# Two softmaxes of cross-attention on one core: the whole program in another order, V's squares through DRAM, and a new division of the last sums

## The chip, the cores and the metric

The kernel runs on one core of a Trainium2 chip. The metric is the device time of one execution in microseconds (us). All data is fp32.

## The reference

Cross-attention with two sets of keys and values. The queries come from `x`; the first 77 rows of `ctx` are text, the last 77 are image rows, and each set has its own projections and its own softmax:

```
x   (2, 2048, 640)     ctx (2, 154, 1024)     20 heads of 32
q    = heads(x @ Wq.T)
text = softmax(q @ heads(ctx[:, :77] @ Wk.T).T / sqrt(32))    @ heads(ctx[:, :77] @ Wv.T)
ip   = softmax(q @ heads(ctx[:, 77:] @ Wk_ip.T).T / sqrt(32)) @ heads(ctx[:, 77:] @ Wv_ip.T)
out  = merge(text + ip) @ Wo.T + bo + x
```

## The kernel before

**Order.** The whole program is emitted by hand from one list of words, `SCHEDULE` (L551 to L616), which `emit` (L622) interprets word by word. Nothing is reordered afterwards: the order of the words is the order in which each engine, and SP's one DMA queue, gets its instructions. An engine executes in order, so a word that waits holds all later words of the same engine. `@n` after a word names its PSUM bank or half.

**Steps.** A step q = 0..9 is a batch (0 to 4 are batch 0, 5 to 9 are batch 1) and a chunk of 128 channels, that is 4 heads. Each step has two units u = 2q and 2q + 1 of 1024 tokens, and each unit three groups s = 0, 1, 2 of 3, 3 and 2 token tiles of 128. The words of a step:

| word | engine | what |
|---|---|---|
| `q.u.h`, `cq.u.h` | PE, ACT | queries of 512 tokens, 5 matmuls (L191); copied to SBUF with the scale (L201) |
| `k`, `v`, `ck`, `cv` | PE, ACT | projections of keys and values (L132), copied |
| `R`s.u | PE | scores of a group against 154 keys (L223), into half of PSUM |
| `K`s.u | ACT | copies the scores to SBUF (L235) |
| `M`, `S`, `E` | DVE, POOL, ACT | maxima (L261), subtraction (L275), exponential (L281) |
| `D`, `N` | DVE, POOL | sums (L288) with their reciprocals (L290), normalisation (L295) |
| `T` | DVE | transpose in squares of 32x32 (L302) |
| `A.q`, `CA.q` | PE, ACT | attend with V (L311), for the whole step; copied into `aT` (L334, L338) |
| `SQ.c`, `VS.q.half` | DVE, SP | V transposed to squares (L142); squares spread over the partitions (L148), 8 DMAs a half |
| `LX.u.h` | SP | block of 512 tokens of `x`, 1.28 MB (L176); batch 1's blocks take 3 slots in turn, in the order of the LX words |
| `LK`, `LQ`, `LO` | SP | weights |

A group thus goes PE, ACT, DVE, POOL, ACT, DVE, POOL, DVE, and `A.q` needs the T of all six groups of its step. An LX into a slot waits for the queries that read the slot last.

**Output projection.** Batch 0's, by 7 products of sums instead of 8 for most of its size, lies among the steps of batch 1: `W` and `G` are sums of operands on POOL (L380, L410), `m`j.i the products j of block i on PE (L477, L487), `cm`j.i adds them on DVE into `acc` (L502, L508); `o`, `co` do the last 128 channels (L457, L467). Four blocks i share the buffers `acc` and `res`, in five parts. A store of a part (L446, L448) is issued right in the `co` or `cm` that completes it, and the fetch of the residual for the same part of the next block (L438, L440) comes one store later, from the list `due`. `LF` fetches the five parts of block 0.

**Tail.** Batch 1's projection follows A.9. It uses 33 products, each in two halves (`F`, 66 words of one matmul, L835), of sums of weights (`V`, 128x128, L813 and L815) and sums of rows of `aT` (`X`, 128x1024, L821). A suffix names the engine: `.d` is DVE, `.p` is POOL. `Y` adds a bank into an output part on DVE (L779, L781), and each part is stored when its last `Y` is done. `p`, `z` and `yz` do the last 128 channels; `LW` and `LA` load weights and the residual.

Of the kernel before, what the change touches and what calls it, by code (L numbers as in the profile page):

```python
# [20 lines left out]
def kernel(  # L21
# [122 lines left out]
    def spread_v(q, half):  # L144

        for g in range(G * half // 2, G * (half + 1) // 2):
            for r in range(G):
                nc.sync.dma_start(  # L148
                    out=v4s[q % 2][r * D : (r + 1) * D, g].rearrange("p k d -> p (k d)"),
                    in_=squares(q)[g * D : (g + 1) * D],  # L150
                )
# [92 lines left out]
    def exponential_of(u, s, ps):  # L244

        n = GROUPS[s][1]
        for g in range(G):
            for t in range(n):
                for x in range(2):
                    nc.scalar.activation(  # L250
                        rows_of(u, s)[:, t * G + g, x],
                        rows_in(ps[g], n)[:, t, x],
                        AF.Exp,
                        bias=maxs[(u, s)][:, t * G + g, x : x + 1],
                    )

    def maxima(u, s, ps=None):
        n = GROUPS[s][1] * G
        mx = small.tile([P, n, 2], F32, tag=f"mx{n}", name=f"mx_{u}_{s}")
        if ps is None:  # L260
            nc.vector.tensor_reduce(mx, rows_of(u, s), AX.X, ALU.max)  # L261
# [23 lines left out]
    def sums(u, s):  # L285
        n = GROUPS[s][1] * G
        den = small.tile([P, n, 2], F32, tag=f"den{n}", name=f"den_{u}_{s}")
        nc.vector.tensor_reduce(den, rows_of(u, s), AX.X, ALU.add)  # L288
# [1 line left out]
        nc.vector.reciprocal(rden, den)  # L290
# [205 lines left out]
    def take_product(m, b, i, ps):  # L496
        part = {2: (0, 0), 1: (0, 0), 5: (1, 1), 7: (1, 1), 3: (0, 1), 6: (0, 1), 4: (1, 0)}[m]
        t = part_in(sums_of(b, i), *part)
        if m in (5, 3, 4, 1 if b else 2):
            for op in range(2):  # L500
# [4 lines left out]
                if b and m == 4:  # L505
                    nc.sync.dma_start(out=in_dram(outT, b, i, *part)[:, op], in_=t[:, op])
        else:
            nc.vector.tensor_tensor(t, t, ps.rearrange("p (op t) -> p op t", op=2), ALU.add)  # L508
# [369 lines left out]
```

## Time and profile before

| | us |
|---|---|
| median of 3 runs (511.25 to 512.14) | 511.52 |
| span of the profiled execution | 509.3 |

The page gives the profiled execution's time as its span alone; the median lies 2.2 above it.

In that execution the engines were busy for this share of the span: PE 97%, DVE 85%, POOL 81%, ACT 48%. PE's matmul rows are pipelined and their ends are modelled. In the rows below, `PE` is the matmul queue, `PEld` its weight loads, `SPq` SP's DMA queue. A row of a timeline has start, duration, engine, line, operation, output and inputs, and the count of instructions run together; in brackets is the idle time of the engine just before, and what ended it. A row of a table of windows has the window and its length, then for each of PE, PEld, DVE, ACT and POOL the busy time and the number of instructions, then the clock granted to PE (1.00 is full), the share of the DMA engines, and GB/s. A row of a group has busy time, mean duration in ns, and idle time ahead with what ended most of it. Line numbers are those of the kernel before.

### The profile page before, as it was taken

The page shows a single profiled execution, that of the slowest core. Times are in us where ns is not written, and L with a number is a line of the kernel's source. Part 1 is how long each engine was busy: PE and PEld are TensorE (multiplying, and loading weights), DVE is VectorE, ACT ScalarE, POOL GpSimd, SP SyncE. Part 2 cuts the span into 40 slices and gives each one's busy share as a digit, 9 for nine tenths or more (in the row PEclk, how much of TensorE's full clock was granted, in tenths as well). Part 3 has the DMA queues.
Part 4 walks back from the last instruction along what each step waited for, and adds up shares of the span by engine and source line. Part 5 has one row for each costly group of instructions (what it writes and reads, how often), then busy time and mean ns, then how long its engine had stood idle before and what let it go on. Part 6 is the DMA issues. An engine that isn't in the chain of part 4 may idle for free.

```text
span 509.3 us, 9862 instructions
## 1 busy us (share of the span) xinstructions
PE 496.4 (97%) x4114; PEld 292.1 (57%) x4114; DVE 431.5 (85%) x401; ACT 242.8 (48%) x423; POOL 414.3 (81%) x176
## 2 busy tenths in 40 slices
PE   9999999999989999999999999996999999999996
PEld 5657557557458556446655565553666576444442
DVE  0078989989987989977995999799299999999986
ACT  1266657577566567654636544663466453100000
POOL 0078999999997979988998899799399999468750
PEclk9999999999999999999999999997999999999999
DMA  8994050502441554577444724534914022310017
GB/s 272 357 287 134 16 136 11 142 3 71 129 148 42 157 192 141 200 238 250 146 134 146 242 62 155 210 106 134 322 30 124 27 82 64 125 62 1 21 62 268
DMA packets 67468, 69.34 MB, mean 136 GB/s; under 512 B 5472, under 2 KB 47200, under 8 KB 67424
## 3 DMA queue, kind: packets, MB, share of 16 engines
q1 hardware_dynamic: 66704, 68.00, 42.5%
q8 instruction: 32, 0.52, 0.4%
q10 hardware_dynamic: 720, 0.72, 0.4%
q14 instruction: 12, 0.10, 0.1%
HBM read 54.94 MB, written 10.49 MB: 128 GB/s over the span
## 4 chain that ended last, share of the span: by engine, by line
PE 69%; DVE 9%; DMA 8%; POOL 8%; ACT 2%; SPq 2%; issue 1%; DVEq 0%; POOLq 0%
PE bank L191 22%; PE bank L835 11%; PE bank L477 8%; PE bank L223 8%; PE bank L311 6%; PE bank L132 6%; POOL pb L275 5%; PE bank L457 4%; DMA x<-in_x_dram 3%; DVE pb L302 3%; POOL pb L295 3%; PE bank L487 2%; DVE mx L261 2%; DVE den L288 2%; DMA wo_ct<-in_L_xattn_Wo_dram 2%; DMA aT<-in_L_xattn_Wk_ip_dram 2%
## 5 line engine op out<-in xcount | busy, mean ns | idle before, releaser
L275 POOL TENSOR_TENSOR pb<-pb,mx 128x1848 f32<-128x1848 f32 (+1 forms) x60 | 175.6, 2946 | 42.4 <-DVE mx L261 42.3
L295 POOL TENSOR_TENSOR pb<-pb,rden 128x1848 f32<-128x1848 f32 (+1 forms) x60 | 175.6, 2948 | 15.4 <-DVE rden L290 15.1
L191 PE MATMUL bank<-x,wq 128*128 128x512 f32 x400 | 182.5, 606 | 4.8 <-DMA x<-in_x_dram 4.5
L261 DVE TENSOR_REDUCE mx<-pb 128x24 f32<-128x1848 f32 (+1 forms) x60 | 109.3, 1837 | 34.4 <-ACT pb L235 34.4
L191 PEld LDWEIGHTS bank<-x,wq 128*128 128x128 f32 x400 | 75.0, 193 | 92.8 <-issue 82.8
L235 ACT COPY pb<-bank 128x462 f32<-128x462 f32 (+1 forms) x240 | 101.9, 534 | 54.2 <-PE bank L223 53.6
L281 ACT ACTIVATE pb<-pb 128x1848 f32<-128x1848 f32 (+1 forms) x60 | 94.9, 1583 | 68.0 <-POOL pb L275 67.8
L288 DVE TENSOR_REDUCE den<-pb 128x24 f32<-128x1848 f32 (+1 forms) x60 | 110.2, 1836 | 16.3 <-ACT pb L281 16.3
L302 DVE STREAM_TRANSPOSE pb<-pb 128x1920 f32<-128x1920 f32 (+1 forms) x60 | 114.6, 1924 | 0.9 <-POOL pb L295 0.9
L223 PEld LDWEIGHTS bank<-kT,qT 32*128 32x128 f32 x1280 | 47.1, 185 | 27.6 <-issue 20.2
L223 PE MATMUL bank<-kT,qT 32*128 32x154 f32 x1280 | 58.8, 307 | 1.6 <-issue 1.3
L311 PE MATMUL bank<-pb,v 32*32 32x512 f32 x1600 | 55.5, 597 | 0.7 <-ACT pb L235 0.7
L132 PE MATMUL bank<-wo_ct,aT 128*128 128x154 f32 x320 | 46.8, 301 | 0.4 <-DMA aT<-in_L_xattn_Wk_ip_dram 0.3
L132 PEld LDWEIGHTS bank<-wo_ct,aT 128*128 128x128 f32 x320 | 44.3, 192 | 4.7 <-issue 3.5
L311 PEld LDWEIGHTS bank<-pb,v 32*32 32x32 f32 x1600 | 29.8, 103 | 22.3 <-issue 10.1
L201 ACT ACTIVATE qT<-bank 128x512 f32<-128x512 f32 x40 | 23.5, 599 | 29.3 <-PE bank L191 29.2
L457 PE MATMUL bank<-aT,wo_ct 128*128 128x512 f32 x80 | 36.3, 595 | 0.0
L477 PE MATMUL bank<-aT,wo_ct 128*128 128x256 f32 x128 | 32.3, 386 | 0.0
L477 PEld LDWEIGHTS bank<-aT,wo_ct 128*128 128x128 f32 x128 | 23.6, 190 | 7.6 <-issue 4.4
L502 DVE SCALAR_TENSOR_TENSOR acc<-bank,bo_sb,acc 128x256 f32<-128x256 f32 x32 | 13.6, 466 | 14.9 <-PE bank L487 14.8
L457 PEld LDWEIGHTS bank<-aT,wo_ct 128*128 128x128 f32 x80 | 15.0, 190 | 16.8 <-issue 16.4
L781 DVE TENSOR_TENSOR x<-x,bank 128x512 f32<-128x512 f32 x36 | 23.1, 678 | 1.0 <-PE bank L835 0.9
(71 smaller groups left out, 343.0 us busy)
## 6 DMA issues: line engine op xcount, KB each, us to landing
x<-in_x_dram SPq DMA_DIRECT2D x20, 1280.0 KB, 8.4
out_dram<-acc SPq DMA_DIRECT2D x20, 256.0 KB, 2.6
x<-in_x_dram SPq DMA_DIRECT2D x18, 256.0 KB, 5.4
acc<-in_x_dram SPq DMA_DIRECT2D x16, 256.0 KB, 3.7
out_dram<-x SPq DMA_DIRECT2D x15, 256.0 KB, 2.3
v<-vS SPq DMA_DIRECT2D x160, 20.0 KB, 2.6
wq<-in_L_xattn_Wq_dram SPq DMA_DIRECT2D x9, 320.0 KB, 5.3
aT<-in_L_xattn_Wk_dram SPq DMA_DIRECT2D x5, 512.0 KB, 4.5
```

The source lines that it names most:

```text
L132: nc.tensor.matmul(keys_in(out), loaded[n][:, k, :], cT[:, k, :, t, :], start=(k == 0), stop=(k == NCC - 1))
L191: nc.tensor.matmul(pq, wqs[q % 3][:, k, :], xs[place_of(u, h)][:, k, :], start=(k == 0), stop=(k == NC - 1),)
L223: nc.tensor.matmul(ps[g][:, ts(t, 2 * L)], qTs[(u, h)][g * D : (g + 1) * D, ts(st, P)], kT[g * D : (g + 1) * D, c, b].rearrange("p t l -> ...
L235: nc.scalar.copy(keys_of(u, s)[:, :, g], ps[g][:, : n * 2 * L].rearrange("p (n l) -> p n l", n=n))
L261: nc.vector.tensor_reduce(mx, rows_of(u, s), AX.X, ALU.max)
L275: nc.gpsimd.tensor_tensor(rows_of(u, s), rows_of(u, s), maxs[(u, s)].unsqueeze(3).to_broadcast([P, n, 2, L]), ALU.subtract)
L281: nc.scalar.activation(e, e, AF.Exp)
L288: nc.vector.tensor_reduce(den, rows_of(u, s), AX.X, ALU.add)
L295: nc.gpsimd.tensor_tensor(rows_of(u, s), rows_of(u, s), rdens[(u, s)].unsqueeze(3).to_broadcast([P, n, 2, L]), ALU.mult)
L302: nc.vector.transpose(p, p)
L311: nc.tensor.matmul(pa[r][g * D : (g + 1) * D, :], v4s[q % 2][rows, g, k, :], zones[rows, :, g, k, :], start=(k == 0), stop=(k == NK - 1),)
L477: nc.tensor.matmul(part, w_of[m][:, kp, op], t_of(m, b, i)[:, kp], start=(op == kp == 0 and m in (1, 2, 5)), stop=(op == 1 and kp == 1 and ...
```

## The change

1. **A new `SCHEDULE`**, 1064 words for 969. All words of PE and ACT are the same; their order, and which words lie between which, is new all through.
2. **Reciprocals, stores, fetches as words.** `D` is the sums alone and `I` the reciprocal. `st.i.part` and `fe.i.part` are a store and a fetch of batch 0's projection; `co` and `cm` no longer issue them. `LF` moves from the first words to behind A.2.
3. **V's squares through DRAM.** `VW.q` writes the 128x160 square to a DRAM tile of its own, and `VS.q`, 4 DMAs where 16 were, reads it spread over the partitions. There are four square buffers instead of seven. SP issues 187 DMAs instead of 297.
4. **The sums of the tail** have other engines: nine X go from DVE to POOL (I, L, V, G, F, J, W, D, M) and two from POOL to DVE (E, Q), so that POOL has 19 of 25; eight of V's go from DVE to POOL and seven the other way.
5. `E` and `M` have branches for a form without `K` or `S`. All 60 `K` and 60 `S` are in the list, so each group takes the form that it had.

The diff, cut to its core:

```diff
+    dram = ctx.enter_context(tc.tile_pool(name="dram", bufs=1, space=bass.MemoryType.DRAM))
+    scr = [dram.tile([P, LP], F32, name=f"scr_{n}") for n in range(NP)]
...
-    vS0 = [const.tile([P, LP], F32, name=f"vS0_{n}") for n in range(2)]
-    vS1 = const.tile([P, NC, LP], F32, name="vS1")
+    vS = [const.tile([P, LP], F32, name=f"vS_{n}") for n in range(4)]
...
     def squares(q):
         b, c = divmod(q, NC)
-        return vS1[:, c] if b else vS0[c % 2]
+        return vS[2 * b + c % 2]
...
-    def spread_v(q, half):
-
-        for g in range(G * half // 2, G * (half + 1) // 2):
-            for r in range(G):
-                nc.sync.dma_start(
-                    out=v4s[q % 2][r * D : (r + 1) * D, g].rearrange("p k d -> p (k d)"),
-                    in_=squares(q)[g * D : (g + 1) * D],
-                )
+    def write_v(q):
+        nc.sync.dma_start(out=scr[q], in_=squares(q))
+
+    def spread_v(q):
+
+        for r in range(G):
+            nc.sync.dma_start(
+                out=v4s[q % 2][r * D : (r + 1) * D].rearrange("p g k d -> p g (k d)"),
+                in_=scr[q].rearrange("(g d) l -> d g l", g=G),
+            )
...
     def sums(u, s):
...
+    def invert(u, s):
+        n = GROUPS[s][1] * G
         rden = small.tile([P, n, 2], F32, tag=f"rden{n}", name=f"rden_{u}_{s}")
-        nc.vector.reciprocal(rden, den)
+        nc.vector.reciprocal(rden, dens[(u, s)])
...
     def store(b, i, part):
...
-        if b == 0:
-
-            for f in due:
-                fetch(*f)
-            due[:] = [(i + 1, part)] if i + 1 < NHB else []
...
     def store_last(ps, b, i):
...
-        store(b, i, "last")
...
-        if m in (6, 7, 2 if b else 1) or m == 4 and not b:
-            store(b, i, part)
...
+        elif k == "VW":
+            write_v(x)
+        elif k == "st":
+            store(0, x, PARTS[y])
+        elif k == "fe":
+            fetch(x, PARTS[y])
```

Of the list, the places that the prediction speaks of, before and after. Ahead of A.1:

```diff
-"M0.4 v.2.0@1 T1.3 S0.4 q.5.1@3 cv.2.0 K1.4 T2.3 cq.6.0 S2.4 M1.4 E0.4 A.1@1 cq.5.1 D0.4 S1.4 E2.4 "
+"R1.4@1 I1.3 N1.3 T0.3 K1.4 M1.4 S1.4 T2.3 cv.2.0 S0.4 LK.12 LK.11 VW.1 T1.3 E2.4 E1.4 D1.4 q.5.1@3 "
+"cq.5.1 I1.4 N1.4 q.6.0@1 D2.4 cq.6.0 VS.1 E0.4 D0.4 I0.4 A.1@1 N0.4 T1.4 CA.1 I2.4 R0.5@0 v.2.1@4 K0.5 "
```

Ahead of A.4:

```diff
-"q.10.1@4 S0.9 K1.9 M2.9 M1.9 S2.9 E0.9 q.11.0@5 SQ.4 LX.12.0 LO T2.8 VS.4.0 S1.9 E2.9 D0.9 q.11.1@2 "
-"T1.8 N0.9 E1.9 VS.4.1 D2.9 cq.11.0 cq.10.1 D1.9 N2.9 R0.10@1 cq.11.1 R2.10@0 K0.10 T0.9 N1.9 "
-"q.12.0@4 LX.12.1 K2.10 VS.5.0 T2.9 W0 T1.9 R1.10@0 cq.12.0 M0.10 A.4@1 K1.10 LX.14.0 LX.13.1 LQ.8 "
+"LQ.6 N0.9 LO T1.8 SQ.4 LX.12.0 E1.9 N2.9 D1.9 I1.9 cq.11.0 VW.4 R2.10@0 T0.9 T2.9 N1.9 VS.4 K0.10 W0 "
+"T1.9 K2.10 LX.12.1 M0.10 S0.10 q.12.0@4 cq.12.0 M2.10 R1.10@0 K1.10 A.4@1 CA.4 q.12.1@0 M1.10 S2.10 "
```

Ahead of A.7:

```diff
-"M1.15 m4.1 E2.15 D0.15 S1.15 q.17.0@3 T0.14 G5.2 E1.15 co.2 N0.15 cm4.1 cq.16.1 D1.15 R1.16@1 "
-"cq.17.0 LX.18.0 VS.7.1 R0.16@0 K1.16 D2.15 q.17.1@4 N1.15 K0.16 T0.15 N2.15 M0.16 VS.8.1 R2.16@0 "
-"q.18.0@7 K2.16 T1.15 G7.2 S0.16 T2.15 LX.18.1 M2.16 LX.19.0 A.7@0 LX.19.1 E0.16 VS.8.0 M1.16 S2.16 "
+"D0.14 M0.15 m7.1 R1.15@0 cm2.2 N2.14 T2.14 I0.14 K1.15 q.17.0@5 N1.14 S0.15 E0.15 cm7.1 m4.1 q.16.1@4 "
+"o.2@1 T1.14 N0.14 M1.15 S1.15 M2.15 S2.15 T0.14 st.1.1 D0.15 I0.15 N0.15 cm4.1 E1.15 D1.15 cq.17.0 "
+"E2.15 fe.2.1 cq.16.1 R1.16@1 D2.15 I1.15 N1.15 co.2 G7.2 R0.16@0 I2.15 LX.18.0 N2.15 T0.15 VS.8 K1.16 "
+"M1.16 T1.15 K0.16 S1.16 q.17.1@4 st.1.2 cq.17.1 M0.16 S0.16 R2.16@0 T2.15 K2.16 M2.16 S2.16 E1.16 D1.16 "
+"VS.7 I1.16 q.18.0@7 cq.18.0 st.1.3 E0.16 D0.16 I0.16 N1.16 A.7@0 T1.16 m5.2@7 cm5.2 CA.7 N0.16 LX.18.1 "
```

The start of the tail:

```diff
-"V.E.0.p N1.19 T0.19 p.1@4 cm4.3 LA N2.19 T1.19 p.3@6 V.H.0.d T2.19 V.O.0.p V.C.0.p V.A.0.p V.P.0.d "
-"V.G.0.d V.P.1.d A.9@0 V.M.0.d V.U.0.d V.Q.0.d V.T.0.d V.U.1.d V.T.1.p V.J.0.d V.U.2.d V.D.0.d "
-"X.B.d@0 V.X.0.d V.B.0.d V.X.1.p V.M.1.d V.X.2.d X.A.d@1 CA.9 X.I.d@2 F31.1@0 F31.0@1 X.L.d@3 F0.1@0 "
-"X.U.d@4 z.0 V.I.0.d X.S.d@5 F25.0@2 z.3 X.V.d@6 F0.0@1 V.X.3.d Y0.1.11 V.X.4.p F7.1@3 V.S.0.p yz.3 "
-"X.E.p@7 z.2 Y6.0.10 Y0.0.11 F23.1@0 Y2.1.31 F20.0@2 yz.2 V.S.1.p F23.0@1 Y0.1.01 X.Q.p@8 Y6.0.11 "
+"cm4.3 I2.19 N2.19 T1.19 p.1@4 T2.19 V.P.1.p V.G.0.d V.U.0.d V.Q.0.d V.X.0.d V.X.1.d A.9@0 CA.9 st.3.1 "
+"V.X.2.d V.M.1.d X.A.d@1 V.L.0.d V.T.0.d V.E.0.d F31.1@0 X.I.p@2 X.L.p@3 X.Q.d@8 X.U.d@4 F31.0@1 F0.1 "
+"V.X.3.d z.2 Y0.1.11 F0.0 V.T.1.d st.3.0 F25.0@2 V.H.0.p X.J.p@12 X.E.d@7 z.0 V.C.0.d st.3.3 z.1 st.3.4 "
+"st.3.2 LA V.X.4.d Y6.0.10 V.L.1.p yz.2 X.S.d@5 z.3 yz.3 Y0.0.11 F23.1 V.A.0.d yz.0 F25.1@7 Y6.1.10 "
+"F23.0 Y0.0.01 F20.0 Y6.0.11 Y0.1.01 F7.1@3 Y2.1.31 F20.1 F24.0 F1.1 F4.0@6 Y6.1.11 F1.0 V.N.0.d V.U.1.p "
```

More of the change, by code (lines that the diff above doesn't have):

```diff
@@ L63 @@
     SCALE = 1.0 / float(D) ** 0.5
-    DIRECT = {}
     NP = B * NC
@@ L242, in rows_in @@
         return ps[:, : n * 2 * L].rearrange("p (n t l) -> p n t l", n=n, t=2)
[L244 to L255, printed above, removed]
     def maxima(u, s, ps=None):
@@ L260, in maxima @@
         if ps is None:
-            nc.vector.tensor_reduce(mx, rows_of(u, s), AX.X, ALU.max)
+            nc.vector.tensor_reduce(mx, rows_of(u, s), AX.X, ALU.max, negate=by_rows(u, s))
         else:
@@ L277, in subtract, with exponential, copied, by_rows @@
         )
-    def exponential(u, s):
-        e = keys_of(u, s).rearrange("p n g l -> p (n g) l")
-        nc.scalar.activation(e, e, AF.Exp)
-    rdens = {}
+    def exponential(u, s, ps):
+        if not by_rows(u, s):
+            e = keys_of(u, s).rearrange("p n g l -> p (n g) l")
+            nc.scalar.activation(e, e, AF.Exp)
+            return
+        n = GROUPS[s][1]
+        for g in range(G):
+            for t in range(n):
+                for x in range(2):
+                    row = rows_of(u, s)[:, t * G + g, x]
+                    nc.scalar.activation(
+                        row,
+                        row if copied(u, s) else rows_in(ps[g], n)[:, t, x],
+                        AF.Exp,
+                        bias=maxs[(u, s)][:, t * G + g, x : x + 1],
+                    )
+    def copied(u, s):
+        return f"K{s}.{u}" in planned
+    def by_rows(u, s):
+        return f"S{s}.{u}" not in planned
+    dens = {}
     def sums(u, s):
         n = GROUPS[s][1] * G
-        den = small.tile([P, n, 2], F32, tag=f"den{n}", name=f"den_{u}_{s}")
-        nc.vector.tensor_reduce(den, rows_of(u, s), AX.X, ALU.add)
+        dens[(u, s)] = small.tile([P, n, 2], F32, tag=f"den{n}", name=f"den_{u}_{s}")
+        nc.vector.tensor_reduce(dens[(u, s)], rows_of(u, s), AX.X, ALU.add)
+    rdens = {}
+    def invert(u, s):
+        n = GROUPS[s][1] * G
         rden = small.tile([P, n, 2], F32, tag=f"rden{n}", name=f"rden_{u}_{s}")
-        nc.vector.reciprocal(rden, den)
+        nc.vector.reciprocal(rden, dens[(u, s)])
         rdens[(u, s)] = rden
@@ L440, in fetch @@
             nc.sync.dma_start(out=part_in(acc, *part), in_=in_dram(xT, 0, i, *part))
-    due = []
     def store(b, i, part):
@@ L504, in take_product @@
                 )
-                if b and m == 4:
-                    nc.sync.dma_start(out=in_dram(outT, b, i, *part)[:, op], in_=t[:, op])
         else:
             nc.vector.tensor_tensor(t, t, ps.rearrange("p (op t) -> p op t", op=2), ALU.add)
-        if m in (6, 7, 2 if b else 1) or m == 4 and not b:
-            store(b, i, part)
     slices.extend((i, k) for i in range(NHB) for k in range(NC))
@@ L551 @@
     SCHEDULE = (
[64 rows of a table removed]
[66 rows of a table added]
     ).split()
     late = [tuple(int(x) for x in w.split(".")[1:]) for w in SCHEDULE if w[:2] == "LX"]
+    planned = {w.partition("@")[0] for w in SCHEDULE}
     JOINS = {3: 5, 6: 1, 7: 6, 4: 7}
@@ L636, in emit @@
             square_v(x)
+        elif k == "VW":
+            write_v(x)
         elif k == "VS":
-            spread_v(x, y)
+            spread_v(x)
         elif k == "LX":
@@ L649, in emit @@
                 fetch(0, part)
-        elif k[0] in "KMSEDNT":
+        elif k[0] in "KMSEDINT":
             ps = at[f"R{i}.{x}"]
@@ L653, in emit @@
                 take(x, i, ps)
-            elif k[0] in "ME":
-                direct = (x, i) in DIRECT
-                if k[0] == "M":
-                    maxima(x, i, ps if direct else None)
-                elif direct:
-                    exponential_of(x, i, ps)
-                else:
-                    exponential(x, i)
+            elif k[0] == "M":
+                maxima(x, i, None if copied(x, i) else ps)
+            elif k[0] == "E":
+                exponential(x, i, ps)
             else:
-                dict(S=subtract, D=sums, N=normalise, T=transpose)[k[0]](x, i)
+                dict(S=subtract, D=sums, I=invert, N=normalise, T=transpose)[k[0]](x, i)
         elif k == "q":
@@ L785, in add_part @@
             nc.sync.dma_start(out=outT[ts(m, P), ds(S + i * TB, TB)], in_=t)
-    home = {}
+    home = {step_of(u)[3] * NH + h: xs[place_of(u, h)] for u, h in late[-XROOM:]}
     def finish(k, args, where):
@@ L796, in finish @@
         elif k == "LA":
-            for u, h in late[-XROOM:]:
-                home[step_of(u)[3] * NH + h] = xs[place_of(u, h)]
             (fourth,) = set(range(NHB)) - set(home)
```

104 rows, old and new, of the table SCHEDULE are left out of this document.

## The prediction

> **What bounds the kernel now.** I read the page first, then a table of the span by stages, then the chain and the timelines.
>
> ```profile
> span 509.3 us, 9862 instructions
> PE 496.4 (97%) x4114; PEld 292.1 (57%) x4114; DVE 431.5 (85%) x401; ACT 242.8 (48%) x423; POOL 414.3 (81%) x176
> 140.00:152.80 12.80, 11.48 (x206) 7.55 (x205) 11.40 (x9) 8.51 (x12) 12.80 (x6) 0.96 0.49 147
> 152.80:165.50 12.70, 12.70 (x97) 10.46 (x98) 9.62 (x8) 7.96 (x16) 9.29 (x4) 0.91 0.15 42
> 203.70:216.40 12.70, 11.91 (x96) 5.89 (x106) 11.99 (x10) 7.90 (x15) 12.62 (x6) 1.00 0.57 201
> 343.70:356.40 12.70, 8.85 (x29) 3.81 (x28) 12.67 (x8) 4.57 (x9) 12.37 (x6) 0.73 0.44 134
> 356.40:369.20 12.80, 12.77 (x208) 8.19 (x208) 2.76 (x4) 5.73 (x13) 4.56 (x2) 1.00 0.92 321
> ```
>
> PE is busy 97% of the span: it is the bound, and its words are the same before and after (order apart). Time can come only from stretches in which PE stands or is slow. Three stand out: 140–165, 203–217 and, by far the largest, 343–356 (8.85 busy of 12.70, clock 0.73). DVE and POOL are nearly as full there (12.67, 12.37); only behind the third hole do they stand (2.76 and 4.56 of 12.80), so there they waited for PE and can follow a PE that comes sooner. The chain and the PE queue name the holes:
>
> ```profile
> 150.13 1.32 issue
> 341.48 9.30 DMA x<-in_x_dram
> 350.82 7.34 PE L191 MATMUL bank<-x,wq 128*128 128x512 f32 x10 [3.85 <-DMA x<-in_x_dram]
> 373.94 4.49 PE bank L191 x10
> 358.16 5.45 PE bank L311 x148
> 216.26 5.84 PE L311 MATMUL bank<-pb,v 32*32 32x512 f32 x160 [0.70 <-ACT pb L235]
> 222.77 2.81 PE L191 MATMUL bank<-x,wq 128*128 128x512 f32 x6 [0.67 <-DMA x<-in_x_dram]
> ```
>
> **Load LX.18.0 (the large hole).** It was issued at 341.48, when queries q.17.0 had let go of the slot, took 9.30, and q.18.0 stood 3.85 for it; the queries then ran 7.34 instead of 4.49 at the low clock. That is 3.85 + 2.85 = 6.7. In the new order q.16.1, o.2 and m4.1 are issued between q.17.0 and q.18.0 beside the scores: two pieces of 4.49 (373.94 shows one of that size) and a shorter one more, so that 18.5 us of PE words lie between slot and use, where 7.1 lay (the words' durations in the PE queue, added up). A load of 9.3 fits with 9.2 to spare: **−6.7**. The other late loads keep 10.5 to 12.6 of such room: covered by the same load with 1 us or more to spare; if one took 14, it would cost 2.
>
> **V's squares through memory, and A.4.** Before, each half is 8 DMAs from the squares; now one write and 4 reads. The nearest rows:
>
> ```profile
> 200.88 15.29 SPq L148 DMA_DIRECT2D v<-vS  x16
> out_dram<-acc SPq DMA_DIRECT2D x20, 256.0 KB, 2.6
> v<-vS SPq DMA_DIRECT2D x160, 20.0 KB, 2.6
> 183.84 3.29 POOL L275 TENSOR_TENSOR pb<-pb,mx 128x1848 f32<-128x1848 f32 x1 [2.02 <-DVE mx L261]
> 213.98 2.18 DVE L302 STREAM_TRANSPOSE pb<-pb 128x1920 f32<-128x1920 f32 x1 [0.61 <-POOL pb L295]
> ```
>
> Sixteen issues held SP's queue 15.29, so LX.12.1 behind them was late (0.67 at 222.77), and A.4 ran 5.84 where 358.16 shows 5.45 (0.39). The new chain for A.4 is the square (0.5), a write (2.6, from the larger store), four issues (under 1 each by 15.29/16, together 2 to 4) and a landing (2.6): 7.7 to 9.7, against 8 us of DVE work between SQ.4 and T1.9. It just fits, or costs up to 1.7; I take 0, since the 128x160 write is a third of the store. The 0.70 stood for T1.9, which waited 0.61 for POOL's N1.9; G5.0 is a new word ahead of N1.9, of 1.3 (as at 231.31, below), but it comes ahead of S1.8, where POOL stood 2.02 for DVE, so it costs nothing. I let 0.70, 0.39 and 0.67 all go: **−1.8**. Bounds: −1.8, and +1.2 if the squares are late by 1.7 and G5.0 adds its 1.3.
>
> **Words moved ahead of the last transpose before an attend step.** DVE now has M1.2 before A.0, M1.4 before A.1, M1.16 before A.7; POOL has S2.4 before A.1, G5.1 and S2.12 before A.5, G7.2 before A.7. Queued behind them are the T and N that the attend waits for.
>
> ```profile
> L261 DVE TENSOR_REDUCE mx<-pb 128x24 f32<-128x1848 f32 x40 | 81.7, 2052 | 30.9 <-ACT pb L235 30.9
> L275 POOL TENSOR_TENSOR pb<-pb,mx 128x1232 f32<-128x1232 f32 x20 | 45.1, 2257 | 3.6 <-DVE mx L261 3.6
> 231.31 1.29 POOL L410 TENSOR_TENSOR x<-aT 128x512 f32<-128x512 f32 x1
> 101.95 3.56 DVE L302 STREAM_TRANSPOSE pb<-pb 128x1920 f32<-128x1920 f32 x2
> 106.59 1.92 PE L311 MATMUL bank<-pb,v 32*32 32x512 f32 x49
> 347.28 3.55 DVE L302 STREAM_TRANSPOSE pb<-pb 128x1920 f32<-128x1920 f32 x2
> 225.86 3.29 POOL L295 TENSOR_TENSOR pb<-pb,rden 128x1848 f32<-128x1848 f32 x1 [1.13 <-DVE rden L290]
> 239.13 1.27 POOL L410 TENSOR_TENSOR aT<-aT,x 128x512 f32<-128x512 f32 x1 [1.39 <-PE bank L477]
> ```
>
> A.1: T ended at 101.95 + 3.56 = 105.51, A.1 began at 106.59, slack 1.08; 2.05 more ahead gives +1.0, and 0.1 for A.0: **+1.1**. A.5: POOL has 1.29 + 2.26 = 3.5 more ahead, and idle spells of 1.13 and 1.39 to put it in; 1.0 is left, half of it under A.5's own slack: **+0.5** (0 to 1.7). A.7: T ended at 350.83; without the hole A.7 would start at 358.16 − 6.7 = 351.46, slack 0.63. M1.16 adds 2.05, so 1.4; G7.2 another 1.3 if POOL is what is late. Against it, DVE's queue was full of words that now lie after A.7: **+1.0** (0 to 2.7). A.9 has V.D, V.P, V.M on POOL for V.E, two sums more of 0.44 (row 463.40 below): **+0.3** (0 to 0.9).
>
> **Reciprocals, stores, fetches as own words.** Same instructions, other places. The first residual fetch (5 DMAs) leaves the crowded start for the time after A.2, where the DMA share is 0.15: 0. Stores no longer sit at the end of cm; a store waiting on SP holds the loads behind it, which is the third rival.
>
> **The tail (after A.9).** Sums X (128x1024) go from DVE to POOL 9 times and back 2 times: 19 on POOL, where 12 were; POOL's tail work becomes 49, DVE's 57 where it was 66.
>
> ```profile
> 438.65 5.52 PE L311 MATMUL bank<-pb,v 32*32 32x512 f32 x160
> 444.50 1.98 PE L835 MATMUL bank<-x,wo_ct 128*128 128x512 f32 x4 [0.34 <-ACT aT L338]
> 458.50 46.85 PE bank L835 x108
> 505.38 0.69 DVE x L781
> L821 DVE TENSOR_TENSOR pb<-aT 128x1024 f32<-128x1024 f32 x6 | 7.2, 1216 | 0.0
> L821 POOL TENSOR_TENSOR pb<-aT 128x1024 f32<-128x1024 f32 x3 | 7.1, 2361 | 0.0
> 472.08 2.02 DVE L815 TENSOR_TENSOR pb<-pb,wo_ct 128x128 f32<-128x128 f32 x1
> 459.55 0.28 DVE L815 TENSOR_TENSOR pb<-pb,wo_ct 128x128 f32<-128x128 f32 x1
> 471.61 2.35 POOL L821 TENSOR_TENSOR pb<-pb 128x1024 f32<-128x1024 f32 x1
> 459.90 3.12 POOL L815 TENSOR_TENSOR pb<-pb,wo_ct 128x128 f32<-128x128 f32 x2 [1.59 <-DVE pb L815]
> 463.40 0.87 POOL L815 TENSOR_TENSOR pb<-pb,wo_ct 128x128 f32<-128x128 f32 x2
> ```
>
> An X costs 1.22 on DVE and 2.36 on POOL. Worse, the engines stop each other: a sum of 0.28 on DVE took 2.02 while POOL's X ran from 471.61 to 473.96, and ended when that ended; two POOL sums that take 0.87 (463.40) took 3.12 beside DVE's. From A.9 to the last sum now: 505.38 + 0.69 − 438.65 = 67.4, of which PE stands little. In the new order, with N2.19's end as zero: X.I holds POOL from 0.45 to 2.8 and keeps DVE's V.G off till 2.8; DVE's run of sums to X.A and V.E lasts to 6.9 and keeps X.L off; X.L ends at 9.2, X.Q (DVE) at 10.4, X.U, V.X.3 and Y0.1.11 at 12.6, V.T.1 at 12.9, or 15.0 if POOL's X.J comes first. PE wants V.T.1 for F25.0 at 1.6 (end of T2.19) + 5.52 + 0.34 + 5 words of 0.87 (2 × 46.85/108) = 11.8. It stands 1.1 to 3.2 there; then F23.0 1.6 to 2.6 for Y0.0.11, behind X.E and X.S; F20.1 and F1.1 0.5 to 1.5. What one stall takes the next need not: 4.3 to 6.3 together, less the 1.2 of such waits before: **+4.0** (3.1 to 5.1), and −1.0 if the sums did not stop each other, since DVE then has 9 us less to do.
>
> The Trainium skill, "SBUF — State Buffer", section "SBUF: two separate sides", says that a VectorE instruction with two SBUF inputs and a GpSimd instruction that reads SBUF take turns at one port pair, the later waiting for the whole of the other. By that the tail is the +4.0; by a view in which both merely run at their speeds it is −1.0.
>
> **The gap at 150.** 1.32 without a wait, then a low clock: 12.8 × 0.04 + 12.7 × 0.09 = 1.7, together 3.0. PE's order there is unchanged, so I keep it; if it goes, −3.0. The Trainium skill, "TensorE: Matmul & The Clock Gate", section "Part 1: The HAM clock gate", wants about 3.4 us of idleness before the clock halves; the windows show 0.96 and 0.91 behind 1.32, so here the measurement decides. By the page the stalls of the tail would cost no clock.
>
> **Sum.** −6.7 − 1.8 + 1.1 + 0.5 + 1.0 + 0.3 = −5.6; tail +4.0; total −1.6. Span 509.3 − 1.6 = 507.7. The median before, 511.52, lies 2.2 over the profiled span; with it **509.9**.
>
> **Rivals.**
> 1. *The engines do not stop each other in the new tail, or the gap at 150 is gone.* For it: in most of the old tail's sums the price is 0.28 and 1.22. Against it: rows 472.08 and 459.90. Tail −1.0: 504.9; gap gone: 506.9; both: 501.9. Chance 0.20.
> 2. *The added words cost their upper ends:* A.5 1.7, A.7 2.7, A.9 0.9, that is 3.4 more: 513.3. For it: DVE and POOL are full up to the hole (12.67, 12.37). Against it: 10 us of DVE idleness right behind it. Chance 0.12.
> 3. *Slower: a load waits on SP behind a store.* In the new list LX.18.0 stands behind st.1.1 (which waits for DVE's cm7.1) and fe.2.1 (which waits for that store). DVE is full there; if cm7.1 comes more than 9.2 us late against m7.1 and the fetch, q.18.0 waits again. From 12 us of lateness on, all of 6.7 is back: 509.9 + 6.7 = 516.6; LX.19.1 is behind stores likewise. For it: the row below, 9.8 of SP's waiting for one such product each nine times. Against it: before, the same stores stood ahead of loads and the hole came from PE's slot. Chance 0.14.
> 4. *The tail's stalls bring the low clock as at 150:* two or three spells of 1.7 give 513.3 to 515.0; chance 0.08.
>
> ```profile
> SPq L448 <- DVE acc L508: 49.8, 9, 9.8
> ```
>
> **How the numbers follow.** Forecast 0.46, with a range of its own of 507.5 to 512.0 (the bounds of the terms, not all at one end). A difference of 0.2% (1.0 us) is about what a measurement of this kernel tells from none: faster is below 510.5, slower above 512.5. Faster: 0.31 of the forecast's 0.46 and rival 1's 0.20: 0.51. Same: 0.13 of the forecast and 0.03 of rival 2: 0.16. Slower: 0.02, 0.09, 0.14 and 0.08: 0.33. The range 501.5 to 516.5 leaves out about half of rival 3, and what is beyond rival 1.
>
> **What would show it.** Right: no DMA wait ahead of L191 near 340–350 and PEclk 1.00 there; no PE wait at A.4; A.1 1 us behind its T; POOL's 128x1024 sums beside DVE sums of 128x128 that take 1 to 2.4, and PE standing over 4 us in the first 15 us after A.9. Wrong: a load's wait ahead of L191 past A.6, a tail under 67 us, or PE waits for T of 2 us and more at A.2, A.3, A.6 or A.8, to which I gave nothing.

## The result, and the profile after

The new kernel is slower: 513.03 us median of 19 runs (511.89 to 515.83) against 510.99 us of the kernel before on the same chips (508.68 to 513.09), a ratio of 1.0048 (95% interval 1.0033 to 1.0063; the ratio and its interval are worked out over all executions, not from the two medians). Forecast was 509.9 against 511.5, 1.6 us less; it is 2.0 us more. In the two profiled executions both halves moved further than forecast: up to A.9 the new kernel won 8.9 us where 5.6 were expected, and the tail (from A.9 to the last Y) lost 12.4, 79.8 for 67.4, where 4.0 were expected. Two of the twelve executions of experiment 7 were slow ones, over 6 us longer than the others, and are left out of its numbers.

The busy time of the engines of the kernel after (span 512.4), and the windows that answer to those of before, with three of its tail (same columns):

```profile
PE 496.0 (97%) x4114; PEld 291.5 (57%) x4114; DVE 434.6 (85%) x393; ACT 243.4 (47%) x423; POOL 432.3 (84%) x184
140.00:152.80 12.80, 11.62 (x213) 7.85 (x212) 11.56 (x10) 8.88 (x13) 12.69 (x5) 1.00 0.80 250
152.80:165.50 12.70, 12.68 (x96) 9.17 (x95) 11.65 (x10) 8.32 (x16) 12.08 (x6) 1.00 0.21 54
343.70:356.40 12.70, 12.70 (x197) 7.48 (x197) 10.88 (x9) 8.38 (x16) 12.70 (x5) 1.00 0.75 255
436.10:450.70 14.60, 10.21 (x22) 3.90 (x22) 14.60 (x17) 1.11 (x5) 11.58 (x6) 1.00 0.05 18
450.70:463.10 12.40, 8.87 (x21) 3.77 (x21) 12.37 (x14) 0.00 (x0) 12.08 (x9) 0.97 0.11 42
463.10:470.50 7.40, 7.40 (x10) 3.09 (x11) 3.79 (x6) 0.00 (x0) 2.34 (x2) 0.58 0.11 38
```

The hole at 343.7 is gone (12.70 of 12.70 at full clock). New holes lie in the tail: PE is busy 10.21 of 14.60 and 8.87 of 12.40, and then runs at 0.58 of its clock for 7.4 us. DVE is busy without a break in the first two. PE's queue in the tail:

```profile
429.74 5.52 PE L325 MATMUL bank<-pb,v 32*32 32x512 f32 x160 [0.27 <-DVE pb L316]
436.10 1.96 PE L840 MATMUL bank<-x,wo_ct 128*128 128x512 f32 x4 [0.84 <-ACT aT L352]
441.90 1.13 PE L840 MATMUL bank<-aT,pb 128*128 128x512 f32 x2 [1.27 <-DVE pb L820]
447.43 1.13 PE L840 MATMUL bank<-aT,pb 128*128 128x512 f32 x2 [0.97 <-DVE x L786]
450.72 1.12 PE L840 MATMUL bank<-aT,pb 128*128 128x512 f32 x2 [2.17 <-DVE x L786]
463.08 2.05 PE L840 MATMUL bank<-aT,pb 128*128 128x512 f32 x2 [3.51 <-DVE acc L786]
464.92 3.62 PE L840 MATMUL bank<-pb,wo_ct 128*128 128x512 f32 x4
```

A.9 starts at 429.74 (438.65 before). The waits are those of F25.0 (1.27), F25.1 (0.97), F23.0 (2.17) and F6.0 (3.51), each for DVE; four products behind the last take 3.62 where four took 1.96. DVE and POOL at the same time (L818 and L820 are sums V, L826 sums X, L786 words Y):

```profile
439.66 2.19 DVE L820 TENSOR_TENSOR pb<-pb,wo_ct 128x128 f32<-128x128 f32 x1
443.63 2.43 DVE L820 TENSOR_TENSOR pb<-pb,wo_ct 128x128 f32<-128x128 f32 x1
451.45 1.39 DVE L786 SCALAR_TENSOR_TENSOR x<-x,bo_sb,bank 128x512 f32<-128x512 f32 x2
456.11 4.78 DVE L820 TENSOR_TENSOR pb<-pb,wo_ct 128x128 f32<-128x128 f32 x2
460.81 1.47 DVE L826 TENSOR_TENSOR x<-aT 128x1024 f32<-128x1024 f32 x1
...
451.36 2.36 POOL L826 TENSOR_TENSOR pb<-aT 128x1024 f32<-128x1024 f32 x1
455.99 2.40 POOL L826 TENSOR_TENSOR pb<-pb 128x1024 f32<-128x1024 f32 x1
458.35 2.39 POOL L826 TENSOR_TENSOR x<-aT 128x1024 f32<-128x1024 f32 x1
```

V.T.1 (439.66) takes 2.19 beside POOL's X.J, V.X.4 (443.63) 2.43 beside X.F. V.U.2 and V.V.0 (456.11) take 4.78 for two, while POOL runs X.V, X.T, X.N and X.C one behind the other: each of the two ends 0.15 behind the end of an X (X.N at 458.39, X.C at 460.74). The two Y words at 451.45, which read a PSUM bank and one tensor in SBUF, take 0.70 each beside an X of POOL: they are not stopped. Y0.0.00, for which F6.0 waits, stands behind V.V.0 and X.B.

### The profile page after: what moved, and what is told of

Read it like the earlier page. It is cut to its first block, busy times and chain, and to the rows that moved or that the text cites. A ratio compares the mean times of both kernels' runs of the same rounds, so it can differ in the third digit from the quotient of the medians.

```text
span 512.4 us, 9752 instructions
## 1 busy us (share of the span) xinstructions
PE 496.0 (97%) x4114; PEld 291.5 (57%) x4114; DVE 434.6 (85%) x393; ACT 243.4 (47%) x423; POOL 432.3 (84%) x184
## 4 chain that ended last, share of the span: by engine, by line
PE 84%; DVE 10%; DMA 3%; issue 1%; SPq 1%; POOL 0%; ACT 0%; ACTq 0%; DVEq 0%; POOLq 0%
PE bank L194 32%; PE bank L226 10%; PE bank L325 10%; PE bank L840 9%; PE bank L483 9%; PE bank L133 8%; PE bank L464 3%; PE bank L493 2%; DVE pb L820 2%; DMA x<-in_x_dram 2%; DMA aT<-in_L_xattn_Wk_ip_dram 2%; DVE pb L316 1%; DVE pb L826 1%; DVE mx L251 1%; DVE den L297 1%
## 5 line engine op out<-in xcount | busy, mean ns | idle before, releaser
L194 PE MATMUL bank<-x,wq 128*128 128x512 f32 x400 | 178.8, 598 | 0.1
L226 PE MATMUL bank<-kT,qT 32*128 32x154 f32 x1280 | 57.3, 306 | 1.5 <-issue 1.2
L133 PEld LDWEIGHTS bank<-wo_ct,aT 128*128 128x128 f32 x320 | 43.0, 188 | 4.3 <-issue 2.7
L325 PEld LDWEIGHTS bank<-pb,v 32*32 32x32 f32 x1600 | 31.2, 103 | 22.6 <-issue 10.0
L840 PE MATMUL bank<-aT,pb 128*128 128x512 f32 x36 | 19.2, 645 | 7.9 <-DVE acc L786 3.5
```

Source lines behind the costliest of these rows:

```text
L133: nc.tensor.matmul(keys_in(out), loaded[n][:, k, :], cT[:, k, :, t, :], start=(k == 0), stop=(k == NCC - 1))
L194: nc.tensor.matmul(pq, wqs[q % 3][:, k, :], xs[place_of(u, h)][:, k, :], start=(k == 0), stop=(k == NC - 1),)
L226: nc.tensor.matmul(ps[g][:, ts(t, 2 * L)], qTs[(u, h)][g * D : (g + 1) * D, ts(st, P)], kT[g * D : (g + 1) * D, c, b].rearrange("p t l -> ...
L325: nc.tensor.matmul(pa[r][g * D : (g + 1) * D, :], v4s[q % 2][rows, g, k, :], zones[rows, :, g, k, :], start=(k == 0), stop=(k == NK - 1),)
```

## The experiments

Theory: the tail lost its time because DVE's sums and POOL's row sums stop each other. Rivals: the time won ahead of A.9 is a debt that falls due in the tail; or the order of the F and Y words makes the waits, whoever does the sums; and for the win, that it was LX.18.0's slot. Ratios are to the kernel before on the same chip. Line numbers are those of each kernel: in those of the experiments L843 and L849 are F, L789 Y, L823 V, L829 X, and L836 the fill.

**1. Whose is the loss?** The new kernel with the old tail (the lists are joined behind N0.19; the stores of block 3 ahead of `LA`):

```diff
-"... V.M.0.p p.2@7 D2.19 T0.19 cm4.3 I2.19 N2.19 T1.19 p.1@4 T2.19 V.P.1.p V.G.0.d ..."
+"... V.E.0.p N1.19 p.2@7 D2.19 T0.19 p.1@4 cm4.3 I2.19 st.3.1 ... LA N2.19 T1.19 V.H.0.d T2.19 V.O.0.p ..."
```

> The new kernel up to the last attention step, then the order and the engines of the old tail. Theory (the 12.4 us that the tail got longer, 79.8 against 67.4, come from its own order and engines): A.9 stays near 430 us and the tail comes back to 67 to 68, so 512.4 - 12 = about 500 of span, and a ratio to the kernel before of about 0.98. Rival (the time won ahead of A.9 is a debt of DVE and POOL that falls due in the tail, whoever does the sums): the tail stays at 75 or more, and the ratio at 0.995 or above.

Measured: 503.43 us, ratio 0.9869 (0.9824 to 0.9914). A.9 starts at 432.21, the tail is 68.2, and PE's waits in it are 0.56 ahead of F31.1 and 0.28 later, none of those above; the window of the tail in which the new kernel stood:

```profile
445.00:457.00 12.00, 11.94 (x28) 5.04 (x27) 11.81 (x19) 0.00 (x0) 10.40 (x7) 1.00 0.17 66
```

The debt falls: with an A.9 6.4 us earlier than before, the old tail is only 0.8 longer than it was. The ratio is a little above the 0.98 expected; in the profile A.9 came 2.5 later than in the new kernel's, by a longer pause in A.3 (last section). This version beats both kernels.

The other way round, the kernel before with the new tail, in two forms. In the first, as the old program gives the late blocks their buffers only at `LA`, which comes later in the new tail, sums ahead of it go to another buffer and are lost; the second gives them from the start.

```diff
-"... V.E.0.p N1.19 T0.19 p.1@4 cm4.3 LA N2.19 T1.19 p.3@6 V.H.0.d T2.19 V.O.0.p ..."
+"... N1.19 T0.19 p.1@4 cm4.3 V.M.0.p N2.19 T1.19 p.3@6 T2.19 V.P.1.p V.G.0.d V.U.0.d ..."
```

> The kernel before up to A.9, then the new tail. Theory: the tail is about 12 us longer on its own, so 511 + 12 = 523, ratio about 1.024. Rival (debt): with the old, later A.9 DVE and POOL are not behind, the tail is 67 to 72 and the ratio 1.00 to 1.01.

> The kernel before up to A.9, then the new tail, with the buffers of the late blocks known from the start as in the new kernel. Theory (the tail is 12 us longer on its own): ratio 1.02 to 1.027 to the kernel before, tail 77 to 80. Rival (debt): ratio 1.01 or below.

Measured: 522.3 us, ratio 1.0236 (1.0186 to 1.0287), tail 76.9; and 520.05 us, ratio 1.0162 (1.0122 to 1.0202), tail 78.4 in its profile. In both the waits at F25.0, F25.1, F23.0 and F6.0 are there, the first three as long as in the new kernel to 0.02 us, though A.9 comes 10 us later. The tail's loss is its own. The second ratio is below the 1.02 to 1.027 expected, though. By ratios the two halves are smaller than by the two profiles: the new order ahead of A.9 is worth about 1.3% (6.7 us), and the new tail costs 1.6% on the old list and 1.8% on the new one (1.0048 against 0.9869), 8 to 9 us; by the intervals each of these is known to about 2 us.

**2. Engines, or order?** Each X on the engine that it had, at its new place:

```diff
-... X.I.p@2 X.L.p@3 X.Q.d@8 ... X.J.p@12 X.E.d@7 ... X.F.p@11 ... X.G.p@10 X.V.p@6 ...
+... X.I.d@2 X.L.d@3 X.Q.p@8 ... X.J.d@12 X.E.p@7 ... X.F.d@11 ... X.G.d@10 X.V.d@6 ...
```

> The new kernel, each sum X on the engine that it had before, at its new place in the list (nine back on DVE, two back on POOL); the sums V as in the new one. Theory (sums of DVE and of POOL with two inputs in SBUF stop each other, and POOL's X of 2.36 hold up DVE's of 0.28): most of the 12 us comes back, PE's waits of 1.27, 2.17 and 3.51 go, ratio 0.982 to 0.990. Rival (the order of the F and Y words makes the waits): the waits stay, and DVE has 9 us more to do: ratio 1.01 or above.

Measured: 517.76 us, ratio 1.0151 (1.0094 to 1.0208); tail 79.1. In this form the theory falls, and the ratio is the rival's. PE's queue has other waits, of 9.2 together where the new kernel has 8.8; two of them:

```profile
446.10 1.12 PE L843 MATMUL bank<-aT,pb 128*128 128x512 f32 x2 [2.08 <-DVE pb L823]
465.84 2.08 PE L843 MATMUL bank<-pb,wo_ct 128*128 128x512 f32 x2 [3.35 <-DVE pb L829]
```

F25.0 waits longer for V.T.1, which is still stopped by POOL (now by X.E; it took 1.77); F18.0 waits for X.V, which now stands in DVE's queue behind Y words. The new order needs its engines: X words stand where POOL would start them early. Engines and order were one design, and undoing one of them alone says nothing on the other; whether the order alone makes the waits is left to the next experiment.

**3. POOL's sums short, all else the same.** Each X of POOL does 128 of its 1024 columns:

```diff
+nc.gpsimd.tensor_tensor(places[w][:, :, :64], ra[:, :, :64], rb[:, :, :64], op)
```

> The new kernel, but each X of POOL does 128 of its 1024 columns only (the rest of the sum is left out; same order, same waits). Theory: DVE's sums V.U.0, V.T.1, V.X.4, V.U.2, V.V.0, which took 1 to 2.4 us beside POOL's X, take 0.28 to 0.7, PE's waits in the tail go, tail 67 to 69, ratio about 0.98. Rival (DVE's own amount and order of work): the same instructions of DVE take as long as in the new kernel and PE's 3.51 wait stays.

Measured: 501.28 us, ratio 0.9833 (0.9788 to 0.9879), tail 67.1, PE's four long waits gone. DVE's V.T.1, then V.U.2 with V.V.0:

```profile
438.55 0.28 DVE L820 TENSOR_TENSOR pb<-pb,wo_ct 128x128 f32<-128x128 f32 x1
449.17 0.76 DVE L820 TENSOR_TENSOR pb<-pb,wo_ct 128x128 f32<-128x128 f32 x2
```

2.19 became 0.28 and 4.78 became 0.76, in the same order of words. PE's only waits from A.9 on are 0.26 at A.9 and 0.31 ahead of F31.1. So it is POOL's time in X that holds DVE's sums of other data, and the order by itself does not make the waits.

**4. The stop by itself.** In the idle first 25 us of the new kernel, sums on buffers that nobody else uses:

```diff
+dve_sums(4)                       # 128x128, two SBUF inputs, alone
+start_pool(); 2 x POOL tensor_tensor 128x1024; dve_sums(4)
+start_pool(); 2 x POOL tensor_tensor 128x1024; 4 x DVE tensor_scalar; 4 x DVE SBUF + PSUM
+start_pool(); 2 x POOL tensor_scalar 128x1024; dve_sums(4)
```

> The new kernel with a measurement ahead of its list, in the first 25 us, where DVE and POOL stand: DVE sums of 128x128 from two SBUF inputs alone; the same beside POOL sums of 128x1024; then DVE's one-input products and sums of a PSUM bank and an SBUF input beside POOL sums; then DVE's two-input sums beside a POOL product with one SBUF input. Theory (an engine's whole instruction keeps the other's out): 0.28 alone; beside POOL's sums the first one takes up to 2.4, or POOL's takes 1 us longer; one-input and PSUM forms stay at 0.2 to 0.35 and POOL's at 2.36. Rival (both are slowed in proportion): each DVE sum takes 0.4 to 0.6 in all forms and POOL's over 2.6.

DVE's queue, then POOL's:

```profile
3.70 1.27 DVE L564 TENSOR_TENSOR acc<-acc,res 128x128 f32<-128x128 f32 x4
5.28 4.49 DVE L564 TENSOR_TENSOR acc<-acc,res 128x128 f32<-128x128 f32 x4 [0.31 <-POOL acc L560]
10.14 4.29 DVE L575 TENSOR_SCALAR acc<-acc 128x128 f32<-128x128 f32 x4 [0.38 <-POOL acc L560]
16.17 1.98 DVE L564 TENSOR_TENSOR acc<-acc,res 128x128 f32<-128x128 f32 x4 [0.38 <-POOL acc L560]
...
5.32 3.97 POOL L569 TENSOR_TENSOR acc<-acc 128x1024 f32<-128x1024 f32 x2
10.19 3.91 POOL L573 TENSOR_TENSOR acc<-acc 128x1024 f32<-128x1024 f32 x2
16.22 5.72 POOL L580 TENSOR_SCALAR acc<-acc 128x1024 f32<-128x1024 f32 x2
```

Four sums take 1.27 alone and 4.49 beside two POOL sums, although no datum joins them. One by one they are 0.29, 1.87, 1.94 and 0.29 us: the first runs, the next two each end 0.15 behind the end of a POOL sum. That is a stop until the other's instruction ends, not a slowing in proportion. The theory was wrong for one-input products: they are stopped as well (0.23, 1.80, 1.94, 0.23). That does not hold for every instruction with one input: the 40 maxima `M` of 128x1848 in the new kernel take 2.02 to 2.08 each, with a POOL instruction beside them or not. The PSUM form began at 14.55, when POOL had ended at 14.10, so this run says nothing on it; the row at 451.45 above does.

The last group does not fit the theory. Beside POOL products with one SBUF input, of 2.87 and 2.77, DVE's four sums took 0.29, 1.01, 0.29 and 0.29: the second was held, but not to the end, and the last two began and ended (17.54 to 18.16) while POOL's first product was still running by its row (16.22 to 19.10). Why is open; no X or V of POOL is such a product. The rule of the Trainium skill, "SBUF — State Buffer", section "SBUF: two separate sides", that of a VectorE instruction with two SBUF inputs and a GpSimd instruction that reads SBUF the later waits for the whole of the other, agrees with the rows of two-input sums beside POOL's sums; this last group does not agree with it.

**5. Two sums moved.**

```diff
-V.U.2.d V.V.0.d
+V.U.2.p V.V.0.p
```

> The new kernel with two of the tail's 62 weight sums and row sums, V.U.2 and V.V.0, on POOL instead of DVE. On DVE they took 4.78 us together beside POOL's run of four X, ahead of the word Y0.0.00 that F6.0 waits for. Theory (each two-input sum of DVE that meets a POOL sum waits for the whole of it, and two such waits make F6.0 late): Y0.0.00 comes over 4 us earlier, the wait of 3.67 ahead of F6.0 goes and with it the slow products behind it; the waits ahead of F25.0, F25.1 and F23.0 stay at 4.9 together; tail 72 to 74, ratio to the kernel before 0.990 to 0.995. Rival (POOL is late then, or X.B is stopped in their stead by as much): the wait at F6.0 stays over 2 us, ratio above 1.000.

Measured: 508.38 us, ratio 0.9943 (0.9915 to 0.9972), tail 73.6. The wait at F23.0 is still there, 2.18. F29.0 and F6.0 on PE, and X.B on DVE:

```profile
458.94 1.99 PE L843 MATMUL bank<-aT,pb 128*128 128x512 f32 x4
...
455.66 3.37 DVE L829 TENSOR_TENSOR x<-aT 128x1024 f32<-128x1024 f32 x1
```

F6.0 follows F29.0 without a wait, though X.B is now stopped in their stead (3.37 instead of 1.47). Two instructions of 0.3 us each on the other engine are worth 1% of the kernel: slower than before becomes faster than before.

**6. Seventeen sums V moved** (I, G, X, M, T, E, C, A, U.2, V.0, S, F to `.p`; DVE keeps five of the sums V, and six X):

> [...] Theory: the waits at F25.0, F25.1 and F23.0 (4.9 together) shrink to under 2 as well, tail 68 to 71, ratio 0.984 to 0.990. Rival (POOL, with 7.7 us more to do, is now late with T, X or the row sums): waits of 5 or more, ratio 0.998 or above.

Measured: 507.95 us, ratio 0.9927 (0.9900 to 0.9954), tail 72.8: between the theory and its rival, and no better than two alone.

```profile
446.13 2.13 PE L843 MATMUL bank<-aT,pb 128*128 128x512 f32 x4 [1.39 <-POOL pb L823]
449.77 1.13 PE L843 MATMUL bank<-aT,pb 128*128 128x512 f32 x2 [1.50 <-DVE x L789]
```

The wait at F25.0 is 0.3 now and F25.1 has none, so the three are under 2 together, as expected; but F23.1 waits 1.39 for POOL's sums, which is the rival's mechanism, and F23.0 still 1.50 for Y0.0.11.

**7. The low clock.** Four products of a zero matrix fill the pause ahead of F6.0:

```diff
-F29.0 F6.0
+F29.0 fill fill fill fill F6.0
```

> The new kernel with four PE products more, of a matrix of zeros, between F29.0 and F6.0, where PE stood 3.51 us and then ran at half its clock for 6.9 us. Theory (half of that loss is the clock, which falls because PE stands): PE has no pause there, the products after it take 0.86 instead of 1.70, 3.2 us come back: ratio to the kernel before about 0.9985 where the new kernel has 1.0048. Rival (the clock falls anyway, or the fall is not paid since DVE's Y words are what is late): ratio 1.003 to 1.007.

Measured: 512.3 us (median of ten), ratio 1.0035 (1.0009 to 1.0062).

```profile
458.31 3.60 PE L836 MATMUL bank<-aT,vS 128*128 128x512 f32 x8
462.93 1.88 PE L849 MATMUL bank<-pb,wo_ct 128*128 128x512 f32 x4
```

In this profile the products behind F6.0 run at full clock (four in 1.88 instead of 3.62) and the tail is 76.7 for 79.8: the 3.1 expected. The ratio does not show it: it is the rival's, and its interval covers the new kernel's own. The profiled execution is the fastest of the ten, and one of two whose mean granted clock is 1.000. In three of the five profiles with the new tail and no fill the low clock came behind F23.0 instead, the pause at F6.0 was 2.0 instead of 3.5, and the tail was 76.9, as long as with the fill. So the 3.1 is what the low clock cost in one profile; where it falls differs between executions, and what it costs the median stays open.

**8. The win: slot or store?** In the kernel before, q.17.0 ahead of q.16.1, and then LX.18.0 also ahead of `co.2` in the list:

```diff
-q.16.1@5 K1.15 cm7.1 ... S1.15 q.17.0@3 T0.14 G5.2 E1.15 co.2 N0.15 cm4.1 cq.16.1 D1.15 R1.16@1 cq.17.0 LX.18.0
+q.17.0@3 K1.15 cm7.1 ... S1.15 q.16.1@5 T0.14 G5.2 E1.15 co.2 N0.15 cm4.1 cq.16.1 D1.15 R1.16@1 cq.17.0 LX.18.0
```

```diff
+q.17.0@3 K1.15 cm7.1 ... S1.15 LX.18.0 q.16.1@5 T0.14 G5.2 E1.15 co.2 N0.15 cm4.1 cq.16.1 D1.15 R1.16@1 cq.17.0
```

> The kernel before with one exchange: q.17.0 ahead of q.16.1, so that 4.4 + 2.6 us of PE work more lie between the slot that it frees and q.18.0. Theory (the hole of 6.7 us is LX.18.0's wait for its slot): the hole goes, A.7 starts 6 to 7 us earlier, ratio about 0.987. Rival (A.7 then waits for its transposes, T ending at 350.8): the gain is under 2 us, ratio 0.996 or above.

> The kernel before with q.17.0 ahead of q.16.1 as in the exchange tried before, and the load LX.18.0 in the list right behind it, ahead of the store of co.2, where SP's queue stood from 333 to 341 for DVE. Theory (it was that store, not the slot, which made the load late): the load is issued at about 333.5, the hole of 6.7 us ahead of A.7 goes, ratio about 0.987. Rival (A.7 then waits for its transposes): gain under 2 us, ratio above 0.996.

Measured: 512.22 us, ratio 1.0043 (1.0017 to 1.0070), the hole as it was; and 506.77 us, ratio 0.9897 (0.9858 to 0.9935). Of the first, DVE's `co.2`, SP's queue, and q.18.0:

```profile
340.36 0.71 DVE L467 SCALAR_TENSOR_TENSOR res<-bank,bo_sb,res 128x512 f32<-128x512 f32 x1
341.09 0.36 SPq L446 DMA_DIRECT2D out_dram<-res  x1
343.43 0.34 SPq L438 DMA_DIRECT2D res<-in_x_dram  x1
343.82 0.45 SPq L176 DMA_DIRECT2D x<-in_x_dram  x1
352.91 6.26 PE L191 MATMUL bank<-x,wq 128*128 128x512 f32 x10 [3.96 <-DMA x<-in_x_dram]
```

The slot was free 10 us ahead of the load: SP stood for DVE's `co.2` to store `res`, then for that store to fetch into `res` again. Of the second, the load and q.18.0, which now follows the scores without a wait; then q.17.0 in the kernel before, and in the new kernel q.17.0 and the load:

```profile
335.43 0.37 SPq L176 DMA_DIRECT2D x<-in_x_dram  x1
350.90 4.56 PE L191 MATMUL bank<-x,wq 128*128 128x512 f32 x10
...
335.51 4.46 PE L191 MATMUL bank<-x,wq 128*128 128x512 f32 x10
...
321.59 4.56 PE L194 MATMUL bank<-x,wq 128*128 128x512 f32 x10
326.18 0.37 SPq L179 DMA_DIRECT2D x<-in_x_dram  x1
```

So in the kernel before two things held the load: the slot, until 339.97, and the store with its fetch, until the load's own issue at 341.48. Freeing the slot alone won nothing; freeing it and putting the load ahead of the store won the hole. The load ahead of the store in the old order of the queries was not tried; by these rows it could go only 1.5 us earlier. In the new kernel the load goes at 326.18, when q.17.0 has just ended (326.15): there the slot decides, and no store does.

**9. V's squares straight from SBUF**, at the places of the new list (16 DMAs for a write and four reads). As the squares of batch 1 are written over before they are spread there, their contents are those of other steps; the DMAs are all there.

```diff
-VW: write to DRAM; VS: 4 reads
+VS: 16 DMAs vS -> v
```

> The new kernel with the squares of V spread straight from SBUF by 16 DMAs a step, as before, at the places of the new list. Theory (the way through DRAM frees SP's queue: 4 issues of 0.7 to 1.3 us where 16 took 15): loads behind the squares come late, and 1 to 4 us are lost at q.12.1 or later: ratio 1.006 to 1.013. Rival (no one waits for SP there): the same as the new kernel, 1.003 to 1.006.

Measured: 519.34 us, ratio 1.0141 (1.0102 to 1.0181). A.9 starts 8.1 later than in the new kernel; A.4 and q.19.1 by PE's queue:

```profile
214.35 7.34 PE L325 MATMUL bank<-pb,v 32*32 32x512 f32 x160
393.19 8.82 PE L194 MATMUL bank<-x,wq 128*128 128x512 f32 x20 [2.67 <-DMA x<-in_x_dram]
```

A.4 takes 7.34 for 5.52, for squares that arrive late (its weight loads wait for them four times, 0.44 to 0.63 each), and A.7 takes 7.33. The load that is 2.67 late stood on SP behind 16 issues that took 11.36, as the theory has it, though far behind q.12.1. So the way through DRAM is worth 5 us by the ratios (1.0141 against 1.0048), in the new order, which spreads the squares late.

## Why the prediction was wrong

**The direction, by one step: the walk through the tail ended too early.** It gave +4.0; the profiles show 79.8 − 67.4 = +12.4, the ratios 8 to 9. As far as it went its waits were right: 4.3 to 6.3 up to F1.1, measured 1.27 + 0.97 + 2.17 = 4.4 (F25.1 waits, which I had not named, in place of F20.1 and F1.1). The 1.2 that I took off for such waits before stands in no row: PE's only wait in the old tail is the 0.34 ahead of F31.1. The mechanism was right too (experiments 3 and 4). But I stopped at F1.1, 25 us into the tail, although the list shows a second run of DVE sums (V.N.0, V.U.2, V.V.0, X.B) beside four X of POOL in a row, ahead of the Y word that F6.0 needs. That wait, which the sum had at nothing, is 3.5, and the low clock behind it 7.4 × 0.42 = 3.1. Another 0.5 lies ahead of F31.1 (0.84 for 0.34), the remaining 0.9 right behind the waits. Experiment 5 takes the wait at F6.0 away, and the kernel becomes faster than the one before.

**The low clock in the tail** was rival 4, with 1.7 a spell and a chance of 0.08. It came, once, for 3.1 in the profile; other profiles of the same tail have it elsewhere (experiment 7). I had weighed the rule on pauses of 3.4 us that the Trainium skill gives ("TensorE: Matmul & The Clock Gate", section "Part 1: The HAM clock gate") against a pause of 1.3 at 150, and applied neither to a wait I had not found.

**The large hole, −6.7:** the forecast came, and by the room that it counted: the load goes 18.2 us ahead of q.18.0 (18.5 forecast), which follows at once, and A.7 starts at 348.87. What was wrong is the reading of the old list. I took 341.48 for the moment at which q.17.0 gave up the slot; the slot was free at 339.97, and the last 1.5 were a store and a fetch on SP, which would have held the load even with the slot free (experiment 8). It is rival 3's mechanism, already at work in the kernel before; I held it against the new list and did not look for it in the old one. The size is that of one profile, too: in three others with this hole it is 5.2 to 5.7, since q.18.0 runs 6.2 to 6.3 there and not 7.34.

**A.4, −1.8:** right. A.4 runs 5.52 without a wait ahead (that is all 160 of its products; the 5.45 of the forecast is a row of 148). From the square at 205.72 to the last landing at 211.11 it is 5.4, less than the 7.7 to 9.7 allowed. Experiment 9 shows that it is the way through DRAM that makes it fit.

**Words moved ahead of an attend step, +2.9 (A.0, A.1, A.5, A.7, A.9):** wrong, measured 0.3. DVE's transposes and PE's queue at A.1, and the transpose ahead of A.7:

```profile
102.83 3.55 DVE L316 STREAM_TRANSPOSE pb<-pb 128x1280 f32<-128x1280 f32 x2
106.49 2.09 PE L325 MATMUL bank<-pb,v 32*32 32x512 f32 x48
...
346.30 1.50 DVE L316 STREAM_TRANSPOSE pb<-pb 128x1280 f32<-128x1280 f32 x1
```

At A.1 the last transpose ends 0.1 before A.1, at A.7 1.1 before. Ahead of A.1 it ended at 105.51 in the old kernel and ends at 106.38 now, so 2.05 more ahead of it cost 0.9, which the slack of 1.08 took; I had added the whole length to the old end. Only A.9 waits, 0.27. Rival 2, the upper ends of these terms, is out.

**The gap at 150, kept at 3.0:** the pause came (1.18 for 1.32), the low clock did not (1.00 in both windows), 1.8 less than forecast. A longer A.3, with a pause of 0.65 in it, took 1.2 of it back: from its first product to the next query words it is 12.0 (182.38 to 194.40), where it was 10.8 (184.44 to 195.25). Both pauses differ between executions of one list (last section), so what they gave this pair of profiles is at least in part luck.

Together: −6.7 − 1.8 + 0.3 − 1.8 + 1.2 = −8.8 of the −8.9 up to A.9, for −5.6 forecast, and +12.4 for +4.0 behind it. The first miss was in the change's favour, so the whole looks closer than its parts.

## What to carry to other kernels

Where DVE and POOL both add tensors in SBUF, moving a sum to POOL is not free for DVE: price each short DVE sum that meets a long POOL sum at the rest of the long one, and look above all at what is queued behind it; small sums go to the engine that already runs the long ones. A walk through a new order goes to its end, or the part not walked gets a bound of its own. And when a load is late, look at its buffer and at what stood ahead of it on its queue: here freeing one of them alone won nothing.
